# Layer 0 of a four-layer image kernel: two output blocks of a step joined, and the stage's last stores issued from three engines

## The chip, the cores and the metric

The kernel runs on one core of a Trainium2 chip, in one launch. The metric is the device time in microseconds. Several executions are timed and the median is given; one further execution is recorded by the hardware profiler.

## What is computed

The input is a batch of 4 images with 16 channels and 512 x 512 pixels. Four layers follow one another. The change is in layer 0, which is a window transformer block:

```python
x = x + depthwise3x3(x, pos_w) + pos_b
win = windows(affine(x), 8, 8)                 # 64 positions per window
q, k, v = split(win @ qkv_w.T + qkv_b)         # 2 heads of 8
out = softmax(q * 8**-0.5 @ k.T) @ v
x = x + (out @ proj_w.T + proj_b)              # back to image order
h1 = gelu(affine(x) @ fc1_w.T + fc1_b)         # 16 -> 64, exact gelu
x = x + (h1 @ fc2_w.T + fc2_b)                 # 64 -> 16
```

Layer 1 quantizes this x (for which it needs the largest absolute value), convolves it 3x3, normalizes it over the batch and clips it. Layer 2 is two 3x3 convolutions with a residual, layer 3 a 3x3 convolution with a two-layer pointwise network and a residual. Layers 1 to 3 are not touched.

## The kernel before

**Layer 0.** `window_attention` works in 64 steps (`STEPS`), numbered n. A step holds, for each of the 4 images (u) and each of 4 strips of rows (vv), eight 8x8 windows side by side: 512 positions. The 128 partitions are four quads of 32; a quad is a strip with two 16-channel halves. A pair of steps (2k, 2k+1) fills one tile `xo` of outputs, 128 columns wide, which is then stored to `x1` in DRAM, the input of layer 1.

All of PE, DVE, ACT and SP run in the order in which the program is written (a manual schedule); POOL is left to the framework. SP issues all DMAs of this stage: the input tiles (`load`), the turned keys (`turn_keys`, L318) and the stores (`_store_block`, L96). In a step the program goes through attention (`scores` L359, `attend` L378 and L383, `divide`, `values` L346), then `queries` of the next step, then `project` (L402, its sum on DVE at L407), and then the last part, which the change is in. There 52 places are filled in turn:

- every third place from the fifth on is a `hidden` (L416): four matmuls of 32x32 tiles for one image and strip, numbered q = 0 to 15 with u = q // 4, into bank 4 + q % 3, followed by the gelu on ACT (L421) into a tile `hid`;
- the other places are `depthwise` of step n + 2 (L295): four matmuls of 32x32 tiles for one tap of one image, into banks 0 to 3. The last two steps have none of it, as there is no step n + 2;
- `output` (L427): when the four hidden tiles of an image are there, four matmuls of 128x32 tiles with fc2 into bank 7, then an add of y on DVE into `xo` (L429) and, in odd steps, `store`: a maximum over xo on DVE (L438) and the store DMAs of that image.

`output` of image 0 stands behind hidden 5, that of image 1 behind hidden 9, that of image 2 behind the 52 places and after `position`, and that of image 3 in the next step, behind its first `scores`. `hid` has 8 buffers, used in turn. In the code:

```python
hids.append(hidden(y, q, n))
if q in (5, 9):
    output(y, xo, hids[q - 5 : q - 1], q // 4 - 1, n)
...
output(y, xo, hids[8:12], 2, n)
last = (y, xo, hids[12:], U - 1, n)
```

A PE instruction waits in order: if one waits for a semaphore, what is written behind it waits as well. In float32 each matmul shows as two records in the trace.

**The end of layer 0.** After step 63 the largest values are reduced on DVE and POOL (L523, L525), a bound is made of them, and every engine loads the resulting flag (L534) and branches: if the bound does not hold, a safer form of layer 0 (`attention_block`) would be run instead. With this input it is not. An odd step stores 16 DMAs for each image; in the last row of steps three of them are split in two, so step 63 has 19 for each image, 76 in all. Layer 1 begins with loads of `x1` (`_load_pairs`, L891), which need these stores.

Of the kernel before, what the change touches and what calls it, by code (L numbers as in the profile page):

```python
# [1 line left out]

# [9 lines left out]
F32 = mybir.dt.float32  # L12
BF16 = mybir.dt.bfloat16
AF = mybir.ActivationFunctionType
ALU = mybir.AluOpType
# [9 lines left out]
P = 128  # L25
# [6 lines left out]
WS = 8  # L32
# [51 lines left out]
        nc.sync.dma_start(part[:, at : at + m, :], src[:, a : a + m, :])  # L84


def _store_block(nc, x1, src, b, r0, cols):

    n = WS // 2
    s, m = divmod(r0 // 2, M)  # L90
    parts = [(1, m, s, 0, n), (0, m + 1, s, 0, n)]
    if m + n == M and s < S - 1:
        parts[1:] = [(0, m + 1, s, 0, n - 1), (0, 0, s + 1, n - 1, 1)]
    for r, mm, ss, at, k in parts:
        part = 32 * b + C * r
        nc.sync.dma_start(  # L96
            x1[mm : mm + k, part : part + C, ss, cols].rearrange("m c x -> c m x"),
            src.rearrange("c (m r) x -> c m r x", r=2)[:, at : at + k, 1 - r],
        )
# [53 lines left out]
def window_attention(ctx: ExitStack, tc, xw, x1, hots, m, v, peak):  # L153
# [14 lines left out]
    nc = tc.nc  # L168
    U = V = 4
    BW = 64  # L170
    NJ = BW // WS
    N = NJ * T
    XW = 2 * BW
    SR = H // 8
    NQ = W // XW
    STEPS = SR // WS * NQ * 2
# [7 lines left out]
    def bank(i):  # L184
        return pairs[i // 2][:, i % 2, :] if i < 4 else singles[i - 4]

    def quad(i):
        return slice(32 * i, 32 * i + 32)
# [82 lines left out]
    px = ctx.enter_context(tc.tile_pool(name="w0x", bufs=2))  # L271
# [12 lines left out]
    def by_window(ap):  # L284
        return ap.rearrange("p (j a x) -> p a j x", a=WS, x=WS)
# [29 lines left out]
    def turn_keys(y, vv):  # L315
        for u in range(U):
            for w in range(2):
                nc.sync.dma_start(  # L318
                    y2[32 * u + C * w : 32 * u + C * w + C, vv, :, w, :],
                    y[32 * vv + C * w : 32 * vv + C * w + C, u, :].rearrange(  # L320
                        "p (j t) -> p j t", t=T
                    ),
                )
# [17 lines left out]
    def values(k, n):  # L341

        vv, jl = k // 2, 4 * (k % 2)
        b = bank(4 + 2 * (k % 2))
        for jj in range(4):
            nc.tensor.transpose(  # L346
                b[:, P * jj : P * jj + P],
                y2[:, vv, jl + jj].rearrange("p w t -> p (w t)"), m("ident"),
            )
        t = px.tile([P, 4, P], F32, tag="yt", name=f"yt{n}_{k}", bufs=3)  # L350
        nc.vector.tensor_copy(t.rearrange("p j c -> p (j c)"), b)  # L351
        return t

    def scores(k, n):

        vv, jl = k // 2, 4 * (k % 2)
        for jj in range(4):
            for u in range(U):
                nc.tensor.matmul(  # L359
                    bank(u)[:, P * jj : P * jj + P],  # L360
                    y2[quad(u), vv, jl + jj].rearrange("p w t -> p (w t)"),
                    g[quad(u), vv, jl + jj].rearrange("p h t -> p (h t)"),
                    start=True, stop=True,
                )
        e = px.tile([P, U, 4, P], F32, tag="e", name=f"e{n}_{k}", bufs=3)
        for i in range(2):
            nc.scalar.activation(  # L367
                e[:, 2 * i : 2 * i + 2].rearrange("p u j t -> p u (j t)"),
                pairs[i], AF.Exp,
            )  # L370
        return e

    def attend(e, yt, k):

        b, d = bank(4 + 2 * (k % 2)), bank(5 + 2 * (k % 2))
        for jj in range(4):
            for u in range(U):
                nc.tensor.matmul(  # L378
                    b[quad(u), P * jj : P * jj + P], yt[:, jj, quad(u)], e[:, u, jj, :],
                    start=True, stop=True,  # L380
                )
        for u in range(U):
            nc.tensor.matmul(  # L383
                d[quad(u)], own, e[:, u].rearrange("p j t -> p (j t)"),
                start=True, stop=True,
            )

    def divide(k, n):
        vv, jl = k // 2, 4 * (k % 2)
        b, d = bank(4 + 2 * (k % 2)), bank(5 + 2 * (k % 2))  # L390
        r = px.tile([P, 512], F32, tag="r", name=f"r{n}_{k}")
        nc.scalar.activation(r, d, AF.Ln)
        nc.scalar.activation(r, r, AF.Exp, scale=-1.0)  # L393
        nc.vector.tensor_tensor(
            o[:, vv, jl : jl + 4].rearrange("p j h t -> p (j h t)"), b, r, ALU.mult
        )

    def project(y):
        for h in range(NH):
            for u in range(U):  # L400
                for vv in range(V):
                    nc.tensor.matmul(  # L402
                        bank(4 + u)[quad(vv)], wo[h][quad(u)], o[quad(u), vv, :, h, :],
                        start=h == 0, stop=h == 1,
                    )
        for u in range(U):
            nc.vector.scalar_tensor_tensor(  # L407
                y[:, u], bank(4 + u), pb, y[:, u], ALU.add, ALU.add
            )

    def hidden(y, q, n):

        u, vv = q // 4, 3 * q % 4
        b = bank(4 + q % 3)
        for k in range(4):
            nc.tensor.matmul(  # L416
                b[quad(k)], fc1[quad(vv), quad(k)], y[quad(vv), u, :],
                start=True, stop=True,
            )
        hd = px.tile([P, N], F32, tag="hid", name=f"hid{n}_{u}_{vv}", bufs=8)  # L420
        nc.scalar.activation(hd, b, AF.Gelu, bias=f1b)  # L421
        return vv, hd

    def output(y, xo, hids, u, n):
        b = bank(7)
        for vv, hd in hids:
            nc.tensor.matmul(b[quad(vv)], m("fc2"), hd, start=True, stop=True)  # L427
        at = BW * (n % 2)
        nc.vector.tensor_tensor(  # L429
            xo[:, u, :, at : at + BW].rearrange("p a (j x) -> p a j x", x=WS),  # L430
            by_window(b), by_window(y[:, u]), ALU.add,
        )
        if n % 2:
            store(xo, n // 2, u)

    def store(xo, k, u):
        i, cb = divmod(k, NQ)
        nc.vector.tensor_reduce(  # L438
            peak[:, U * k + u : U * k + u + 1], xo[:, u], AX.XY, ALU.max,
            apply_absolute_value=True,  # L440
        )
        for vv in range(V):
            for w in range(2):
                r = SR * (2 * vv + w) + WS * i
                _store_block(
                    nc, x1, xo[32 * vv + C * w : 32 * vv + C * w + C, u], u, r,
                    slice(XW * cb, XW * cb + XW),
                )

    ctx.enter_context(  # L450
# [16 lines left out]
    last, xo = None, None  # L467
    for n in range(STEPS + 1):
        if n < STEPS:
            nc.scalar.preload_act_table_set("natural_log_exp_and_others")  # L470
            yts = {0: values(0, n)}
            es = {0: scores(0, n)}
        if last:

            output(*last)
        if n == STEPS:
            break
        for k in range(1, 8):
            es[k] = scores(k, n)
            attend(es[k - 1], yts[k - 1], k - 1)  # L480
            yts[k] = values(k, n)
            divide(k - 1, n)
            if k == 3:
                nc.vector.tensor_reduce(
                    most[:, n : n + 1], ys[n], AX.XY, ALU.max, apply_absolute_value=True
                )
            if k % 2 and n + 1 < STEPS:
                turn_keys(ys[n + 1], k // 2)
        if n + 1 < STEPS:
            queries(ys[n + 1], 0)  # L490
        attend(es[7], yts[7], 7)
        divide(7, n)
        if n + 1 < STEPS:
            queries(ys[n + 1], 1)
        y = ys.pop(n)
        project(y)

        ahead = n + 2 < STEPS
        if ahead and n % 2 == 0 and n // 2 + 2 < STEPS // 2:
            xts[n // 2 + 2] = load(n // 2 + 2)  # L500
        if n % 2 == 0:
            xo = px.tile([P, U, WS, XW], F32, tag="xo", name=f"xo{n}", bufs=1)


        hids, taken = [], [0] * U
        for i in range(13 * 4):
            q, rest = divmod(i - 4, 3)
            if i >= 4 and rest == 0 and q < 16:
                hids.append(hidden(y, q, n))
                if q in (5, 9):  # L510
                    output(y, xo, hids[q - 5 : q - 1], q // 4 - 1, n)
            elif ahead:
                depthwise(n + 2, taken[i % 4], i % 4)
                taken[i % 4] += 1
        if ahead:
            ys[n + 2] = position(n + 2)
        output(y, xo, hids[8:12], 2, n)
        last = (y, xo, hids[12:], U - 1, n)

# [810 lines left out]
```

## Time and profile before

| | |
|---|---|
| median of 3 executions | 6609.31 us (6609.27 to 6616.03) |
| the profiled execution | 6619.37 us, span 6617.5 us |
| mean granted TensorE clock | 0.98 |
| PE busy | 6388.5 us (97%) |
| ACT busy | 4209.4 us (64%) |
| DVE busy | 3192.7 us (48%) |
| POOL busy | 5.9 us |
| DMA issues for stores to x1 (L96) | 2096 on SP, median 0.42 us each, 1.7 us to landing |
| matmuls of fc2 in layer 0 (L427) | 2048 records, median 617 ns |

Durations and places below come from the profiled execution, which took 10.1 us longer than the median of the three runs. "Busy" of PE is the time in which at least one matmul is in the array; many small tiles can be in it together, so a busy PE may still be partly idle. A line of the timeline gives the start, the length, the engine, the line of the program, the operation with its tiles, and how many instructions were merged; in square brackets stand the idle time ahead of it and what ended it. "Issue" there means that no semaphore of the trace explains the idle time.

### The profile page before, as it was taken

To read this page: it belongs to the slowest core of one execution; us is meant where nothing else is said; L and a number is where in the kernel's file an instruction comes from. 1 tells how busy PE (TensorE), PEld (TensorE's weight loads), DVE (VectorE), ACT (ScalarE), POOL (GpSimd) and SP (SyncE) were. 2 spreads that over 40 slices of the span, in tenths; PEclk is the share of its full clock that TensorE was granted. 3 is DMA by queue.
4 is the path that set the end of the run, shared out by engine and by line. 5 is a ranking of instruction groups with operands and counts; after the bars stand their busy time and mean duration, and the time that the engine had idled before them with its cause. 6 is when DMAs were issued, how large, how long until landed. Compare 5 with 4: busy or idle time off the path is not lost. (4 is left out here: it accounts for less than half of the span.)

```text
span 6617.5 us, 317160 instructions
## 1 busy us (share of the span) xinstructions
PE 6388.5 (97%) x146976; PEld 3295.4 (50%) x146976; DVE 3192.7 (48%) x4640; ACT 4209.4 (64%) x5738; POOL 5.9 (0%) x25
## 2 busy tenths in 40 slices
PE   8999999999999999999996689999999999999998
PEld 5555555555555555555553344444444444444443
DVE  3444444444444444444445944444444444444444
ACT  5777777777777777777774545554555555555553
POOL 0000000000000000000000000000000000000000
PEclk9999999999999999999997789999999999999999
DMA  3333232333333333333324722222222222222221
GB/s 81 65 67 76 57 75 59 73 60 72 60 72 60 72 61 70 62 70 62 70 44 165 275 85 79 79 79 76 76 78 78 78 78 75 75 79 79 79 63 47
DMA packets 544391, 515.30 MB, mean 78 GB/s; under 512 B 349008, under 2 KB 480208, under 8 KB 514384
## 3 DMA queue, kind: packets, MB, share of 16 engines
q1 hardware_dynamic: 542768, 494.52, 28.6%
q8 instruction: 1154, 18.91, 1.2%
q14 instruction: 181, 1.48, 0.1%
q10 hardware_dynamic: 288, 0.39, 0.0%
HBM read 225.87 MB, written 134.48 MB: 54 GB/s over the span
## 5 line engine op out<-in xcount | busy, mean ns | idle before, releaser
L1117 PE MATMUL tb<-y,mat 32*32 32x512 f32 x16384 | 1684.6, 597 | 14.0 <-ACT hid L1123 7.5
L1123 ACT ACTIVATE hid<-tb,vec 128x512 f32<-128x512 f32 x1280 | 877.0, 687 | 1231.0 <-PE tb L1117 1205.6
L1125 DVE TENSOR_SCALAR hid<-tb,vec 128x512 f32<-128x512 f32 x768 | 576.8, 751 | 1173.9 <-PE tb L1117 860.5
L367 ACT ACTIVATE e<-pair 128x1024 f32<-128x1024 f32 x1024 | 992.4, 1021 | 225.7 <-PE pair L359 225.0
L295 PE MATMUL pair<-x,taps 32*32 32x512 f32 x18432 | 968.1, 606 | 1.9 <-ACT y L306 1.3
L416 PE MATMUL bank<-y,fc_e 32*32 32x512 f32 x8192 | 878.4, 607 | 3.7 <-ACT hid L421 3.1
L421 ACT ACTIVATE hid<-bank,f1b 128x512 f32<-128x512 f32 x1024 | 679.3, 686 | 298.3 <-PE bank L416 284.6
L351 DVE COPY yt<-bank 128x512 f32<-128x512 f32 x512 | 353.7, 691 | 905.8 <-PE bank L346 905.5
L1117 PEld LDWEIGHTS tb<-y,mat 32*32 32x32 f32 x16384 | 500.3, 103 | 406.0 <-issue 242.8
L359 PE MATMUL pair<-g,y 32*128 32x128 f32 x16384 | 652.2, 285 | 39.7 <-ACT e L367 38.7
L908 PE MATMUL tb<-z,cw 32*32 32x512 f32 x12864 | 643.8, 603 | 4.0 <-ACT z L1054 3.4
L359 PEld LDWEIGHTS pair<-g,y 32*128 32x128 f32 x16384 | 541.4, 186 | 185.9 <-ACT e L367 108.8
L908 PE MATMUL tb<-x,cw 32*32 32x512 f32 x12480 | 632.0, 597 | 1.5 <-ACT z L1054 1.5
L908 PE MATMUL tb<-h,cw 32*32 32x512 f32 x12672 | 628.6, 601 | 1.8 <-ACT z L1054 1.5
L295 PEld LDWEIGHTS pair<-x,taps 32*32 32x32 f32 x18432 | 459.0, 103 | 288.8 <-issue 183.7
L908 PE MATMUL tb<-q,cq 32*32 32x512 bf16 x12672 | 446.5, 436 | 122.1 <-ACT q L987 97.9
L378 PE MATMUL bank<-e,yt 128*32 128x128 f32 x16384 | 555.3, 276 | 0.9 <-ACT r L393 0.9
L383 PE MATMUL bank<-e,hot 128*32 128x512 f32 x4096 | 534.4, 592 | 0.0
L1131 PE MATMUL tb<-hid,mat 128*32 128x512 f32 x4096 | 498.5, 605 | 0.9 <-DVE o L1137 0.9
L378 PEld LDWEIGHTS bank<-e,yt 128*32 128x32 f32 x16384 | 417.7, 109 | 108.1 <-DVE yt L351 52.8
L429 DVE TENSOR_TENSOR xo<-bank,y 128x512 f32<-128x512 f32 x256 | 177.1, 692 | 546.2 <-PE bank L427 544.4
L346 PEld LDWEIGHTS bank<-mat,y 128*128 128x128 f32 x2048 | 215.2, 141 | 430.2 <-issue 376.5
(150 smaller groups left out, 6608.8 us busy)
## 6 DMA issues: line engine op xcount, KB each, us to landing
tx<-x SPq DMA_DIRECT2D x128, 1024.0 KB, 5.2
x<-in_xw_dram SPq DMA_DIRECT2D x32, 2600.0 KB, 9.9
y<-y SPq DMA_DIRECT2D x2048, 32.0 KB, 2.2
xi<-x SPq DMA_DIRECT2D x1024, 64.0 KB, 2.8
out_dram<-o SPq DMA_DIRECT2D x64, 1024.0 KB, 4.1
x<-xo SPq DMA_DIRECT2D x2000, 32.0 KB, 1.7
tx<-x SPq DMA_DIRECT2D x4, 768.0 KB, 4.2
x<-xo SPq DMA_DIRECT2D x48, 24.0 KB, 1.6
```

The costliest lines, as they stand in the source:

```text
L295: nc.tensor.matmul(bank(u)[quad(vv)], taps[quad(u), tap, :], xts[n // 2][quad(u), vv, dy : dy + WS, at : at + BW], start=tap == 0, stop=ta ...
L359: nc.tensor.matmul(bank(u)[:, P * jj : P * jj + P], y2[quad(u), vv, jl + jj].rearrange("p w t -> p (w t)"), g[quad(u), vv, jl + jj].rearra ...
L367: nc.scalar.activation(e[:, 2 * i : 2 * i + 2].rearrange("p u j t -> p u (j t)"), pairs[i], AF.Exp,)
L378: nc.tensor.matmul(b[quad(u), P * jj : P * jj + P], yt[:, jj, quad(u)], e[:, u, jj, :], start=True, stop=True,)
L383: nc.tensor.matmul(d[quad(u)], own, e[:, u].rearrange("p j t -> p (j t)"), start=True, stop=True,)
L416: nc.tensor.matmul(b[quad(k)], fc1[quad(vv), quad(k)], y[quad(vv), u, :], start=True, stop=True,)
L421: nc.scalar.activation(hd, b, AF.Gelu, bias=f1b)
L908: nc.tensor.matmul(p[i][_quad(j)], weights[_quad(i), side, dx, :], src[side][_quad(i), j, dx : dx + W], start=side == 0 and dx == 0, stop= ...
L1117: nc.tensor.matmul(p[_quad(c)], w1[_quad(b), 1 - par, 32 * c : 32 * c + 32], inner(ys(mm + par))[_quad(b), s, :], start=True, stop=True,)
L1123: nc.scalar.activation(hd, p, AF.Relu, bias=v("l3_b1"))
L1125: nc.vector.tensor_scalar(hd, p, v("l3_b1"), 0.0, ALU.add, ALU.max)
L1131: nc.tensor.matmul(out_bank[_quad(b), :], w2[:, par], hd, start=par == 0, stop=par == 1)
```

## The change

`output` now takes two images at once where it is called within the 52 places: behind hidden 10, for image 1 (hidden 4 to 7) into bank 6 and then image 0 (hidden 0 to 3) into bank 7, eight matmuls in a row. The two adds, and in odd steps the two stores, follow in that order. The outputs of images 2 and 3 stay where they were. `hid` gets 12 buffers. The stores of the last pair of steps (k = 31, so those of step 63) take their issuing engine from a cycle of SP, ACT and POOL; all other stores stay on SP.

```diff
-def _store_block(nc, x1, src, b, r0, cols):
+def _store_block(nc, x1, src, b, r0, cols, queues=None):
...
-        nc.sync.dma_start(
+        (next(queues) if queues else nc.sync).dma_start(
...
-        hd = px.tile([P, N], F32, tag="hid", name=f"hid{n}_{u}_{vv}", bufs=8)
+        hd = px.tile([P, N], F32, tag="hid", name=f"hid{n}_{u}_{vv}", bufs=12)
...
-    def output(y, xo, hids, u, n):
-        b = bank(7)
-        for vv, hd in hids:
-            nc.tensor.matmul(b[quad(vv)], m("fc2"), hd, start=True, stop=True)
+    def output(y, xo, hids, us, banks, n):
+
+        for k, (vv, hd) in enumerate(hids):
+            nc.tensor.matmul(
+                bank(banks[k // 4])[quad(vv)], m("fc2"), hd, start=True, stop=True
+            )
         at = BW * (n % 2)
-        nc.vector.tensor_tensor(
-            xo[:, u, :, at : at + BW].rearrange("p a (j x) -> p a j x", x=WS),
-            by_window(b), by_window(y[:, u]), ALU.add,
-        )
-        if n % 2:
-            store(xo, n // 2, u)
+        for u, i in zip(us, banks):
+            nc.vector.tensor_tensor(
+                xo[:, u, :, at : at + BW].rearrange("p a (j x) -> p a j x", x=WS),
+                by_window(bank(i)), by_window(y[:, u]), ALU.add,
+            )
+            if n % 2:
+                store(xo, n // 2, u)
+
+
+    queues = itertools.cycle((nc.sync, nc.scalar, nc.gpsimd))
...
-                    slice(XW * cb, XW * cb + XW),
+                    slice(XW * cb, XW * cb + XW), queues if k == STEPS // 2 - 1 else None,
...
-                if q in (5, 9):
-                    output(y, xo, hids[q - 5 : q - 1], q // 4 - 1, n)
+                if q == 10:
+
+
+                    output(y, xo, hids[4:8] + hids[0:4], (1, 0), (4 + 8 % 3, 7), n)
...
-        output(y, xo, hids[8:12], 2, n)
-        last = (y, xo, hids[12:], U - 1, n)
+        output(y, xo, hids[8:12], (2,), (7,), n)
+        last = (y, xo, hids[12:], (3,), (7,), n)
```

In step 63 the 38 stores of images 1 and 0 go 13 to SP, 13 to ACT and 12 to POOL; those of image 2 go 6, 6 and 7, those of image 3 go 7, 6 and 6. In the order of ACT's program the first 13 stand between gelu 10 and gelu 11, the others behind gelu 15.

More of the change, by code (lines that the diff above doesn't have):

```diff
@@ L1 @@
+import itertools
 from contextlib import ExitStack
```

## The prediction

> **What bounds the kernel now.** I read the page's first part, then stages cut from the span, then the order of instructions around the edited lines. The page names TensorE:
>
> ```profile
> PE 6388.5 (97%) x146976; PEld 3295.4 (50%) x146976; DVE 3192.7 (48%) x4640; ACT 4209.4 (64%) x5738; POOL 5.9 (0%) x25
> ```
>
> Layer 0 runs to about 3560 us, in 64 steps of some 54 us. The page's chain of waits reaches back only into the convolution layers, so it says nothing on this stage. A table by stage does (us, then busy time of PE, PEld, DVE, ACT, POOL; clock; DMA share):
>
> ```profile
> 1000.00:2000.00 1000.00, 989.11 (x21908) 569.49 (x21904) 463.90 (x611) 775.97 (x1035) 0.00 (x0) 1.00 0.32 66
> ```
>
> PE is busy 989 of 1000 us at full clock. Matmul ends are modelled and overlap, so "busy" hides idle array; the starts tell more. The timeline of PE, then of its weight loads, then of DVE, around one step's output blocks:
>
> ```profile
> 1075.24 0.69 PE L416 MATMUL bank<-y,fc_e 32*32 32x512 f32 x4
> 1075.86 1.06 PE L427 MATMUL bank<-hid,mat 128*32 128x512 f32 x8
> 1076.85 0.66 PE L295 MATMUL pair<-x,taps 32*32 32x512 f32 x8
> ...
> 1080.25 1.07 PE L427 MATMUL bank<-hid,mat 128*32 128x512 f32 x8
> ...
> 1086.81 1.06 PE L427 MATMUL bank<-hid,mat 128*32 128x512 f32 x8
> ```
>
> ```profile
> 1074.78 0.23 PEld L416 LDWEIGHTS bank<-y,fc_e 32*32 32x32 f32 x8
> 1075.85 0.16 PEld L427 LDWEIGHTS bank<-hid,mat 128*32 128x32 f32 x8 [0.84 <-issue]
> 1076.85 0.15 PEld L295 LDWEIGHTS pair<-x,taps 32*32 32x32 f32 x12 [0.84 <-issue]
> ```
>
> ```profile
> 1077.01 0.69 DVE L429 TENSOR_TENSOR xo<-bank,y 128x512 f32<-128x512 f32 x1 [4.12 <-PE bank L427]
> ```
>
> Around each L427 block the weight loads stand still for 0.84 us, on both sides, with no semaphore named: the array empties before it goes from 32x32 tiles to 128x32 tiles, and again on the way back. From the block's start to the next small matmul is 0.99 us.
>
> The end of the layer has another bound, SP:
>
> ```profile
> 3516.80 38.39 SPq L96 DMA_DIRECT2D x<-xo  x76
> ...
> 3533.02 0.69 DVE L429 TENSOR_TENSOR xo<-bank,y 128x512 f32<-128x512 f32 x1 [0.88 <-PE bank L427]
> ...
> 3536.12 0.15 DVE L533 TENSOR_SCALAR flag<-bound 128x1 int32<-128x1 f32 x1
> ...
> 3559.76 37.05 SPq L891 DMA_DIRECT2D tx<-x  x13
> ```
>
> The last data are ready at 3533.7 and the flag at 3536.3, but SP issues its 76 stores until 3555.2 (one is 0.42 us, about 0.47 from one to the next, with a few long ones), and layer 1's first load comes 4.6 us after that.
>
> **What the Trainium skill says.** "TensorEngine Tiling (Array Packing)", Key Properties: changing the tiling mode, not merely the tile, drains TensorE. The trace agrees: 0.84 us without weight loads on each side. "DMA: Bandwidth & Descriptors", Issuing engines are not separate DMA queues: DMAs from scalar, sync and gpsimd share the same 16 engines, so several issuers save only the time to initiate. Issue is what binds here (DMA share 0.25 in 3536 to 3560). The same page, Anatomy of one DMA — SWDGE (gpsimd) path, gives about 2.0 us fixed for a GpSimd DMA, most of it the receipt, and its summary table about 1 us to the first byte; no DMA of this trace is issued from POOL, so none here shows it. For ACT the trace has a price: its two loads at the start took 0.40 and 0.45 us, while SP issued too.
>
> **The change, part by part.**
>
> *Blocks.* I call four matmuls of L295 or L416 on one row strip a slot; in two passes each it leaves 8 records. Between the first and second block lie 12 slots, 4.39 us; between second and third 20 slots, 6.56 us. Now the first block goes, 15 more slots run on behind the first 20, then comes one block of eight matmuls, then 17 slots. The fc2 work doesn't vanish: a block of 8 records takes 1.06 us against 0.62 for one, so a pass adds about 0.45, and the four moved matmuls lengthen the other block by two passes, 0.9 us. With p us per slot in an undisturbed run, the old stretch is 4.39 + 6.56 = 10.95 and the new one 15p + (4.39 + 5p) + 0.9: the saving is 5.66 - 20p. All hangs on p. The two distances above give (6.56 - 4.39)/8 = 0.271, saving 0.24. The run ahead of the first block, from hidden 2 (1072.57) to hidden 5 (1074.79), gives 2.22/9 = 0.247, saving 0.72. The depthwise prelude at full clock (28.3 to 34.6, 214 records less about 19 in flight at an edge) gives 6.3/195 x 8 = 0.258, saving 0.50. I take the last. The first 62 steps have depthwise work: **31 us** (15 to 45). Drains alone would suggest much more; most of a block's 4.39 us is work that stays.
>
> *Gelu and banks.* Hidden 6 to 10 come without a break, one in 3 x 0.258 = 0.77 us; an L421 gelu is 0.69, so ACT keeps up. hid gets 12 buffers: hidden 0 to 10 fit. The block's first half writes bank 6, which gelu 8 must have left; its hidden is two hiddens ahead, as gelu 7 was for the old second block. Hidden 11 wants bank 6 again, after DVE's add. Before, the add started 1.15 us after its block and took 0.69: free at +1.84. Hidden 11 comes at 0.99 + 0.9 for the block, plus 0.05 for two slots: +1.94. Cover 0.1 us; I take no wait, at worst 0.1 x 62 = 6 us. If it waits, everything behind it on PE waits. The first add (u = 0) moves behind add u = 1 and its reduction, and the 32 stores of both images go to SP together in odd steps, 15 us of a queue that is next wanted for keys in the following step: nothing. xo is first written later than before, so its old stores are no later cover than they were.
>
> *Step 62* has no depthwise work; there a break holds the gelus up by 3.0 us (3514.87 to 3517.91 in its twin, step 63). One break less, a longer other: **1.5 us** (0 to 3).
>
> *Stores of step 63.* SP gets 26, ACT 25, POOL 25. Worked from the old step 63: gelus come three in 2.74 us, so gelu 10 ends near 3519.7, the block starts near 3519.2, add u = 1 ends near 3521.9 (1.94 + 0.69 after), add u = 0 near 3523.9. ACT then issues 13 stores ahead of gelu 11: 13 x 0.47 to 3528.0. Gelus 11 to 15 end at 3531.3, add u = 2 at 3533.2, add u = 3 at 3536.0, 2.3 us later than now. SP then has 7 stores left, to 3539.3, not the end any more. POOL is: its 25 stores start at 3521.9 and stand ahead of the reduction (L525) that makes the flag. At 1.0 us each, my estimate from the skill's page, they end at 3546.9; the flag takes 1.1 (3535.18 to 3536.27 before), layer 1 another 4.6: 3552.6 against 3559.76, **7 us** saved. At SP's 0.47, 15 us; at 2.0, 18 us lost; even at about 1.3.
>
> **Sum:** 31 + 1.5 + 7 = 39.5. The profiled execution took 6619.4 (span 6617.5), so 6579.9 of it; it stood 10.1 above the median of 6609.3, so about **6570**.
>
> **Rivals.**
> 1. *Work, not drains:* p stays at 0.271, 62 x 0.24 = 15; with 1.5 and 7: 6586. For: it is the pace next to the blocks. Against: the prelude.
> 2. *The wide gain:* p of 0.247 and a POOL as quick as SP: 45 + 3 + 15: 6546.
> 3. *POOL gates:* 2 us a store; 31 + 1.5 - 18: 6595. For: its queue alone holds the flag. Against: the skill's page puts most of the 2 us after issue.
> 4. *Slower:* the add u = 1 is let go only when the whole block is done. It then starts 0.9 later, hidden 11 comes at +2.79 against 1.94, and PE, in order, loses up to 0.85 in each of 62 steps: 53 - 31 - 8.5 = 13 us slower, 6623. It decides from a wait of 0.64 a step (39.5/62). Against: the two halves are waited for apart in the compiled order.
> 5. The output blocks do move in the compiled order, so a change without effect is only the rivals cancelling.
>
> **How the numbers follow.** Forecast 0.42, rival 1 0.20, rival 2 0.15, rival 3 0.13, rival 4 0.07, cancelling 0.03. A measurement can tell about 0.2%, 13 us, so faster means below 6596. Forecast, 1 and 2 lie there, and half of 3: 0.84. Same: half of 3 and the cancelling, 0.09. Slower 0.07. The range runs from just beyond rival 2 to past rival 3: 6543 to 6601.
>
> **What would show it.** Three L427 blocks a step instead of four, one with 16 records; the distance from its start to the third block near 4.39 + 5 x 0.258 + 0.9 = 6.6 us; the step 0.5 us shorter; no wait of L416 on DVE's xo. At the end, POOL's stores spaced near 1 us and layer 1's load about 16.6 us after the last add (now 26.1). If the step is not shorter, p is wrong or bank 6 is late; if the gap at the end is longer than now, it is POOL.

## The result and the profile after

The changed kernel takes 6591.28 us (median of 9 runs, 6583.26 to 6596.14). The kernel before, run beside it, takes 6616.37 us (6609.27 to 6620.79). The ratio is 0.9962 with a 95% interval of 0.9952 to 0.9972: 25 us less. The profiled execution took 6596.14 us (span 6594.3), against 6619.37 (6617.5) before.

TensorE is still what the page names:

```profile
PE 6374.4 (97%) x146976; PEld 3369.2 (51%) x146976; DVE 3195.1 (48%) x4640; ACT 4221.1 (64%) x5738; POOL 18.9 (0%) x50
```

The timeline of PE around the output blocks of one step (start, length, engine, line, operation, count). L428 is the old L427, L417 the old L416, L296 the old L295:

```profile
1074.59 1.92 PE L428 MATMUL bank<-hid,mat 128*32 128x512 f32 x16
...
1081.53 1.06 PE L428 MATMUL bank<-hid,mat 128*32 128x512 f32 x8
...
1084.26 1.07 PE L428 MATMUL bank<-hid,mat 128*32 128x512 f32 x8
```

Three blocks instead of four, the first of 16 records. Its start lies 6.94 us ahead of the next block's. The weight loads of the same place, and the adds on DVE:

```profile
1074.59 0.16 PEld L428 LDWEIGHTS bank<-hid,mat 128*32 128x32 f32 x8 [0.84 <-ACT hid L422]
...
1076.45 0.18 PEld L296 LDWEIGHTS pair<-x,taps 32*32 32x32 f32 x16 [0.84 <-issue]
```

```profile
1075.78 1.49 DVE L433 TENSOR_TENSOR xo<-bank,y 128x512 f32<-128x512 f32 x2 [7.95 <-ACT hid L422]
```

The pause of 0.84 us on each side of a block is as long as before; there is one pair of them less. (The profile books the first one here to the last gelu that the block needs; it is exactly as long as those for which it names no semaphore.) The first add starts 1.19 us after the block, as soon as its half of the block allows, and nothing in the step waits for it.

The end of layer 0, all engines, with what an engine waited for in square brackets:

```profile
3497.95 21.21 SPq L97 DMA_DIRECT2D x<-xo  x26
3497.96 7.36 ACTq L97 DMA_DIRECT2D x<-xo  x13
...
3498.23 6.30 POOL L97 DMA_DIRECT2D x<-xo  x12 [3476.70 <-DVE xo L433]
...
3505.37 1.84 ACT L422 ACTIVATE hid<-bank,f1b 128x512 f32<-128x512 f32 x3 [9.37 <-DMA x<-xo]
3506.11 2.51 PE L417 MATMUL bank<-y,fc_e 32*32 32x512 f32 x16 [5.94 <-ACT hid L422]
...
3513.37 0.69 DVE L433 TENSOR_TENSOR xo<-bank,y 128x512 f32<-128x512 f32 x1 [0.88 <-PE bank L428]
...
3518.19 0.31 POOL L534 PARTITION_ALL_REDUCE ytop<-top  x1
3518.53 0.27 DVE L539 TENSOR_SCALAR bound<-bound,ytop,sized 128x1 f32<-128x1 f32 x1 [3.02 <-POOL ytop L534]
...
3519.09 0.15 DVE L542 TENSOR_SCALAR flag<-bound 128x1 int32<-128x1 f32 x1
```

Three things are to be seen. Twelve stores on POOL take 6.30 us, 0.52 each, about SP's pace. ACT issues its 13 first stores ahead of gelu 11, so the gelus stand still for 9.37 us and PE for 5.94. And the last add ends at 3514.07, the flag at 3519.24, and layer 1's first load starts at 3525.10: 11.0 us after the last add, where it was 26.1.

In stages, by the two traces:

| | before | after | difference |
|---|---|---|---|
| one step (mean of 61) | 54.19 | 53.79 | -0.40 |
| end of the last add | 3533.71 | 3514.07 | -19.6 |
| layer 1's first load | 3559.76 | 3525.10 | -34.7 |
| from there to the end (layers 1 to 3) | 3057.7 | 3069.2 | +11.5 |

In this pair of traces layer 0 gains 34.7 us, near the forecast of 39.5. But layers 1 to 3, which the change doesn't touch, take 11.5 us longer. Where that comes from was the question for the experiments.

### The profile page after: what moved, and what is told of

It reads as the page before. It is cut to its first block, busy times and chain, and to the rows that moved or that the text cites. A ratio compares the mean times of both kernels' runs of the same rounds, so it can differ in the third digit from the quotient of the medians.

```text
span 6594.3 us, 316838 instructions
## 1 busy us (share of the span) xinstructions
PE 6374.4 (97%) x146976; PEld 3369.2 (51%) x146976; DVE 3195.1 (48%) x4640; ACT 4221.1 (64%) x5738; POOL 18.9 (0%) x50
## 5 line engine op out<-in xcount | busy, mean ns | idle before, releaser
L1126 PE MATMUL tb<-y,mat 32*32 32x512 f32 x16384 | 1696.1, 597 | 10.7 <-ACT hid L1132 7.7
L296 PE MATMUL pair<-x,taps 32*32 32x512 f32 x18432 | 963.6, 605 | 2.9 <-ACT y L307 1.3
L417 PE MATMUL bank<-y,fc_e 32*32 32x512 f32 x8192 | 840.5, 607 | 7.3 <-ACT hid L422 6.7
L1126 PEld LDWEIGHTS tb<-y,mat 32*32 32x32 f32 x16384 | 503.5, 103 | 393.6 <-issue 229.3
L360 PE MATMUL pair<-g,y 32*128 32x128 f32 x16384 | 636.9, 284 | 39.5 <-ACT e L368 38.7
L296 PEld LDWEIGHTS pair<-x,taps 32*32 32x32 f32 x18432 | 526.0, 103 | 226.5 <-issue 102.4
L360 PEld LDWEIGHTS pair<-g,y 32*128 32x128 f32 x16384 | 526.6, 186 | 185.3 <-ACT e L368 108.8
```

Source lines behind the costliest of these rows:

```text
L296: nc.tensor.matmul(bank(u)[quad(vv)], taps[quad(u), tap, :], xts[n // 2][quad(u), vv, dy : dy + WS, at : at + BW], start=tap == 0, stop=ta ...
L360: nc.tensor.matmul(bank(u)[:, P * jj : P * jj + P], y2[quad(u), vv, jl + jj].rearrange("p w t -> p (w t)"), g[quad(u), vv, jl + jj].rearra ...
L417: nc.tensor.matmul(b[quad(k)], fc1[quad(vv), quad(k)], y[quad(vv), u, :], start=True, stop=True,)
L1126: nc.tensor.matmul(p[_quad(c)], w1[_quad(b), 1 - par, 32 * c : 32 * c + 32], inner(ys(mm + par))[_quad(b), s, :], start=True, stop=True,)
```

## The experiments

**Each part alone, and both kernels again.** The joined block with all stores on SP:

```diff
-                    slice(XW * cb, XW * cb + XW), queues if k == STEPS // 2 - 1 else None,
+                    slice(XW * cb, XW * cb + XW), None,
```

> The joined block alone; all stores stay on SP. The trace of the changed kernel has a step 0.45 us shorter than before (54.11 to 53.66 us) and layers 1 to 3 11.5 us longer (3069.2 instead of 3057.7 us from the first tx load to the end). If the blocks are worth what the steps show: layer 0 shorter by about 62 x 0.45 = 28 us, the gap from the last add to layer 1's first load as before (26 us) or a little longer. Theory A, the lengthening of layers 1 to 3 comes with the stores on ACT and POOL: they take 3058 us here, in all about 28 us less than before. Theory B, it comes with the new order of blocks: 3069 us, in all about 17 us less. Theory C, it varies from execution to execution: either, and the median some 22 us less. The rival that joining saves nothing: no change of the steps.

The stores on three engines with the old blocks (`hid` with 8 buffers, no joined output):

```diff
-                if q == 10:
-                    output(y, xo, hids[4:8] + hids[0:4], (1, 0), (4 + 8 % 3, 7), n)
+                if q in (5, 9):
+                    output(y, xo, hids[q - 5 : q - 1], (q // 4 - 1,), (7,), n)
```

> The stores of step 63 on three engines alone; output blocks and hid buffers as before. Steps of 54.1 us. The gap from the last add to layer 1's first load was 26.05 us before and 11.04 us in the changed kernel; ACT's stores delay gelus by some 5 us in step 63. So layer 0 ends about 8 to 11 us earlier. Theory A: layers 1 to 3 take 3069 us, in all no gain or up to 3 us lost. Theory B: 3058 us, in all 8 to 11 us less. Theory C: either, median about 4 us less.

The two kernels once more, for the spread of the stages on this chip:

> The kernel before once more, for a second profile. Theories A and B: layers 1 to 3 take 3058 us again, within 1 us. Theory C: they may take up to 3069 us.

> The changed kernel once more, for a second profile. Theories A and B: layers 1 to 3 take 3069 us again, within 1 us. Theory C: they may take down to 3058 us. Layer 0 to the first tx load: 3525 us.

| | time, us | ratio to before | layers 1 to 3 |
|---|---|---|---|
| joined block alone | 6592.68 (6590.66 to 6595.83) | 0.9963 [0.9950, 0.9977] | 3051.2 |
| stores alone | 6617.67 (6609.23 to 6631.06) | 1.0002 [0.9994, 1.0010] | 3068.1 |
| before, once | 6609.51 | | 3054.6 |
| changed, once | 6594.15 | | 3069.3 |

So the joined block alone gains as much as the whole change, 24.5 us of medians. The stores alone bring nothing, although layer 1's first load follows the last add by 11.0 us there too. Layers 1 to 3 take 3051 to 3058 us with the stores on SP and 3068 to 3069 with the stores on three engines.

Two readings go with this table. The stages of a single trace are good to some 5 us: in the second pair of profiles layer 1's first load comes 30.1 us earlier (3523.09 against 3553.14), not 34.7, and layers 1 to 3 take 14.7 us longer, not 11.5. And with all stores on SP the joined block makes the end of layer 0 longer, by its one trace. Counted from the first copy of `yt` in step 63 (L351 before, number 504 counting from 0; "copy 504" below), layer 1's first load comes after 92.1 us with the joined block alone, after 88.0 and 85.0 in the two profiles of before, and after 77.0 and 77.2 in those of the changed kernel.

**What lengthens layers 1 to 3.** Setting the two traces side by side, DVE instruction by instruction, most of the difference comes in jumps of some 0.8 us, fifteen of them (12.2 us together), one every 168.5 us. At these places PE's weight loads pause without a semaphore in both kernels. The first line is of before, the next two of after:

```profile
4118.80 0.13 PEld L1117 LDWEIGHTS tb<-y,mat 32*32 32x32 f32 x5 [1.13 <-issue]
```

```profile
4085.16 0.10 PEld L917 LDWEIGHTS tb<-z,cw 32*32 32x32 f32 x1 [1.23 <-issue]
4085.16 0.12 PEld L1126 LDWEIGHTS tb<-y,mat 32*32 32x32 f32 x3
```

The pause is nearly as long in both. But in the kernel before it falls ahead of a whole group of four L1117 matmuls, one for each strip; in the changed one it falls elsewhere, and of the matmuls of L1126 three start and the fourth comes late. The matmuls of PE behind the pause, before and then after:

```profile
4118.81 0.63 PE L1117 MATMUL tb<-y,mat 32*32 32x512 f32 x4 [0.23 <-issue]
```

```profile
4085.16 0.61 PE L917 MATMUL tb<-z,cw 32*32 32x512 f32 x1 [0.32 <-issue]
4085.16 0.62 PE L1126 MATMUL tb<-y,mat 32*32 32x512 f32 x3
...
4086.04 0.58 PE L1126 MATMUL tb<-y,mat 32*32 32x512 f32 x1
```

In the compiled programs PE's executed instructions are the same in number. But the branch to `attention_block`, which is not entered, has 32646 instructions for PE instead of 32642: with POOL's stores in the program, PE waits for four more semaphores there. All of PE's code for layers 1 to 3 behind it moves by four. (The branch grows by four for the other engines as well.) The theory "place of the code" says that this alone costs the 11 us; the rival "queues" says that stores on POOL or ACT leave something behind. The first kernel for it is the kernel before with one matmul more in the branch that is not entered. It moves PE's code alone. In float32 that is also four instructions, as the trace shows two weight loads and two matmuls for each:

```diff
         nc.tensor.matmul(pk, wk, chunk(xw, k), start=True, stop=True)
+        for _ in range(1 if (i, k) == (0, 0) else 0):
+            nc.tensor.matmul(pk, wk, chunk(xw, k), start=True, stop=True)
```

> The kernel before with one more matmul in the attention branch, which this input never enters: nothing that is executed differs from the kernel before. In the program it moves all of TensorE's code for layers 1 to 3 by four instructions, as much as the changed kernel's branch grew (four waits more, for the POOL stores in it). Theory 'place of the code': layers 1 to 3 (first load of layer 1 to the end) take 3069 us as in the changed kernel, not 3055, and the kernel is 11 to 16 us slower than before, near 6630. Rival 'queues' (stores on the ACT and POOL queues leave something behind that slows layers 1 to 3): no difference from before, 6616 and 3055.

The changed kernel with 15 such matmuls in another function of the same branch, so that together with the four waits 64 instructions are added (4 + 15 x 4); it is called the padded kernel below:

```diff
     def project(xw, o, n, k):
...
+        for _ in range(15 if n == f"{NB-1}_{NC-1}" else 0):
+            nc.tensor.matmul(pp, wp[:, 0], o[:, :, 0, :], start=True, stop=True)
```

> The changed kernel with 15 repeated matmuls in the branch that is not entered, 64 instructions of TensorE's with the four waits, so that the code of layers 1 to 3 lies as in the kernel before, but for 64 instructions; nothing that is executed differs from the changed kernel. 'Place of the code', with a pattern that repeats every 64 instructions: layers 1 to 3 back at 3051 to 3058 us, near 6581 in all. 'Queues': 3069 and 6594 as before.

The changed kernel with stores on two engines, whose branch has its old size of 32642:

```diff
-    queues = itertools.cycle((nc.sync, nc.scalar, nc.gpsimd))
+    queues = itertools.cycle((nc.sync, nc.scalar))
```

> The changed kernel with the stores of step 63 on SP and ACT alone. Without POOL stores the branch has its old size and the code its old place. 'Place of the code': layers 1 to 3 at 3051 to 3058 us; ACT holds 19 stores ahead of gelu 11 instead of 13, about 10 us, so layer 1's first load comes at 3527 to 3531, and the kernel takes 6580 to 6590. 'Queues' (a second hardware queue is enough): 3069, near 6598.

And the changed kernel with 7 matmuls more at the place of the first diff. They bring one wait more, so that the code moves by 4 + 7 x 4 + 1 = 33:

> The changed kernel with 7 repeated matmuls in the branch that is not entered: the code of layers 1 to 3 lies 33 instructions behind that of the kernel before (mod 64), a third place. 'Place of the code': layers 1 to 3 take another time than 3069, somewhere in 3045 to 3075, with TensorE's unexplained stalls at other instructions. 'Queues': 3069.

| | code moved by | layers 1 to 3 | time, us | ratio to before |
|---|---|---|---|---|
| before, one matmul more | 4 | 3066.7 | 6631.19 (6618.38 to 6635.24) | 1.0016 [1.0008, 1.0025] |
| changed, 15 more | 64 | 3054.3 | 6580.81 (6576.38 to 6585.46) | 0.9948 [0.9934, 0.9961] |
| changed, SP and ACT | 0 | 3050.4 | 6582.34 (6575.68 to 6588.47) | 0.9948 [0.9935, 0.9962] |
| changed, 7 more | 33 | 3051.8 | 6575.91 (one run) | |

One matmul that is never executed makes the kernel before slower by 0.16%, with all its stores on SP. Moving the code by 64 takes the changed kernel from 0.9962 to 0.9948 of before; the intervals of these two still touch, so the stage shows it better than the total. "Queues" falls: POOL's stores are all there in the padded kernel.

The totals of layers 1 to 3 mix in something else. Their first 470 to 477 us and their last 127 to 134 us vary from trace to trace, for the same kernel too (474.1 and 470.4 for the first part in the two profiles of before). Between them, from PE's weight load 60,000 to its load 2,000 (counted back from the end of the program), all traces of this document fall into three groups:

| code moved by | kernels | this stretch, us |
|---|---|---|
| 4 | changed (both profiles), stores alone, before with one matmul more | 2465.4 to 2466.4 |
| 0 or 64 | before (both profiles), joined block alone, SP and ACT, padded, and the three kernels further below | 2453.3 to 2454.6 |
| 33 | changed, 7 more | 2447.9 |

The pause moves as the code does. Counted back in the same way, the first one after 4080 us stands ahead of load 58,008 in the kernels whose code lies at its old place, and ahead of load 58,010 in those moved by four, so two loads and their two matmuls earlier. In those moved by 64 it stands ahead of load 57,016, which is 58,008 - 8 x 128 + 32: earlier by 32 loads and their matmuls, but for a whole number of 128 loads. So its places lie on one fixed grid of 128 loads with their matmuls, 256 instructions, over which the code slides. In the kernel moved by 33 no pause longer than 0.85 us is left in this part; why is not shown.

The trace of the kernel before with one matmul more shows the pause in the changed kernel's form:

```profile
4121.60 0.10 PEld L910 LDWEIGHTS tb<-z,cw 32*32 32x32 f32 x1 [1.11 <-issue]
4121.61 0.11 PEld L1119 LDWEIGHTS tb<-y,mat 32*32 32x32 f32 x3
```

The groups of weight loads from 4080 to 6400 us carry the same sign. These are the rows of `tb<-z,cw` of before, of after and of before with one matmul more (busy and mean, then idle time ahead and what ended it); the changed kernel with 15 more has 187.9 idle, 100.2 of it "issue", as before:

```profile
L908 PEld LDWEIGHTS tb<-z,cw 32*32 32x32 f32 x10560 | 221.7, 103 | 188.0 <-issue 100.0 <-DVE x L1084 61.0
```

```profile
L917 PEld LDWEIGHTS tb<-z,cw 32*32 32x32 f32 x10598 | 225.0, 103 | 205.4 <-issue 113.7 <-DVE x L1093 61.0
```

```profile
L910 PEld LDWEIGHTS tb<-z,cw 32*32 32x32 f32 x10583 | 225.1, 103 | 204.5 <-issue 112.3 <-DVE x L1086 61.0
```

These rows don't show the loss itself: the pause is booked to the load that ends it, and the row of `tb<-y,mat` falls from 330.4 us of idle time before to 316.7 after. They show which load that is, the same one in the changed kernel and in the kernel before with its code moved by four.

That PE pauses there to fetch instructions is argued and not shown. For it: a stretch of 168.5 us holds 3968 weight loads and as many matmuls, 7936 instructions, which are 31 blocks of 256; and the page lists transfers of the kind "instruction" of 16 KB each:

```profile
q8 instruction: 1154, 18.91, 1.2%
```

The Trainium skill, "Runtime: NRT & Kernel Launch", Instruction fetch mechanics, has the instruction memory refilled in 16 KiB blocks of 256 instructions, and calls the cost of crossing a boundary mostly hidden. The block size fits this trace, and so does the number of transfers: by the page's figure, PE's 146976 weight loads and as many matmuls would fill 1148 blocks, an estimate. If the pause is such a crossing, its cost is not hidden here: which instruction the boundary falls on decides about 12 us of the 2454.

**What holds up step 63.** In the padded changed kernel, images 1 and 0 are stored by SP and POOL only, image 2 by ACT, image 3 by SP and POOL:

```diff
-    queues = itertools.cycle((nc.sync, nc.scalar, nc.gpsimd))
+    pair = itertools.cycle((nc.sync, nc.gpsimd))
+    one = itertools.repeat(nc.scalar)
+    queues = (pair, pair, one, pair)
```

> The changed kernel with the padded branch (code of layers 1 to 3 where it lay before) and another division of step 63's stores: images 1 and 0 on SP and POOL alone, image 2 on ACT, image 3 on SP and POOL. If ACT's 13 stores ahead of gelu 11 are what holds up step 63, gelu 11 follows gelu 10 by under 2 us instead of 10, the last add comes 6 to 8 us earlier, SP and POOL carry 19 stores each from the joined block on (19 x 0.51 = 9.7 us) and then 9 or 10 of image 3's (5 us), and layer 1's first load comes 2 to 5 us earlier: about 6577. If gelu 11 waited for something else, no change from the padded kernel: 6581.

It takes 6578.52 us (6575.27 to 6587.18; 0.9944 [0.9931, 0.9958]), which the runs can't tell from the padded kernel. In the trace, gelu 11 and the stores:

```profile
3498.82 18.85 SPq L97 DMA_DIRECT2D x<-xo  x29
...
3499.10 14.43 POOL L97 DMA_DIRECT2D x<-xo  x28 [3478.05 <-DVE xo L433]
...
3501.08 3.19 ACT L422 ACTIVATE hid<-bank,f1b 128x512 f32<-128x512 f32 x5 [4.22 <-PE bank L417]
```

ACT's stores are gone from ahead of gelu 11, which now follows gelu 10 by 4.9 us instead of 10.0. The expected 2 us is missed since gelu 11 then waits for PE, where the joined block (3.64 us here) stands ahead of its hidden layer. From copy 504 the last add ends after 59.6 us instead of 65.1, but layer 1's first load comes after 75.7 instead of 76.3. SP, with 29 stores until 3517.67, has become the last to issue, so ending ACT's hold-up wins almost nothing.

**A second joined block.** Does the gain of the change repeat? Images 2 and 3 in one block at the start of the next step, in the padded changed kernel:

```diff
-        output(y, xo, hids[8:12], (2,), (7,), n)
-        last = (y, xo, hids[12:], (3,), (7,), n)
+        last = (y, xo, hids[8:], (2, 3), (6, 7), n)
```

> The padded changed kernel with images 2 and 3 also in one block, on banks 6 and 7, at the start of the next step. It takes away a block between the hidden layer (32x32 tiles) and the values (128x128), where one change of tile remains: so one drain of about 0.52 us goes each step, 63 x 0.52 = 33 us, if a drain costs PE its gap wherever it stands. The joined block of the change gained 0.45 us a step for a pair of drains, by which ratio 15 us. So 6545 to 6566. Rival: PE waits in the block for gelu 15 or the scores for the adds, and the gain is eaten: 6575 or more. The tail of step 63 gets 2 to 3 us longer, since image 2's stores start later.

It takes 6583.89 us (6582.57 to 6586.89; 0.9953 [0.9939, 0.9967]): nothing gained. The step is 53.78 us, and 53.77 in the padded kernel. The rival holds, though its cause is ACT. PE at the start of a step:

```profile
3390.86 0.66 PE L347 MATMUL bank<-mat,y 128*128 128x128 f32 x4 [0.16 <-ACT hid L422]
3391.49 0.49 PE L360 MATMUL pair<-g,y 32*128 32x128 f32 x4
3392.27 1.16 PE L360 MATMUL pair<-g,y 32*128 32x128 f32 x28 [0.28 <-ACT y L307]
3393.36 1.92 PE L428 MATMUL bank<-hid,mat 128*32 128x512 f32 x16
```

The values wait for the last gelu, which reads bank 4, and the scores for `position` on ACT (L307). On ACT three gelus, L307, a table load and the first exponential follow one another without a gap; from the first of these gelus to the exponential it is 4.66 us in the padded kernel (3387.19 to 3391.85) and 4.67 in this one (3388.86 to 3393.53). At this place ACT sets the pace, and the block that was taken away there had cost nothing.

**Both together.** The second joined block, and images 1 and 0 stored by SP and POOL, 2 and 3 by all three:

> Images 2 and 3 in one block as in the second kernel, and the stores of step 63 for images 1 and 0 on SP and POOL, for 2 and 3 on all three engines. If both effects stand by themselves, 3 to 6 us below the second kernel.

It takes 6579.82 us (6577.33 to 6582.92; 0.9945 [0.9931, 0.9958]), 4.1 below the second joined block alone, as expected, though the two intervals overlap. In the trace layer 1's first load comes 73.3 us after copy 504, against 76.3 in the padded kernel: the shortest end of layer 0, without a measurable gain over that kernel. In the traces of this kernel and of the first of the three, layers 1 to 3 take 3060.7 us, 6.4 more than in the padded one; by the stretches above, all of it lies in their first and last parts, which vary.

The padded kernel, the one with SP and ACT, and the first and last of these three all lie at 0.9944 to 0.9948 of before and aren't told apart. The plainest of them is the changed one with POOL taken out of the cycle. It is clear of the kernel before, and below the changed kernel in the median, though these two intervals touch (0.9935 to 0.9962 and 0.9952 to 0.9972).

## Why the prediction was right, and where not

The forecast was 6570 us, with 6543 to 6601; the result is 6591, faster, as the forecast said. Its sum of 39.5 us stands against 25 of medians (23 by the two traces), and rivals 1 and 3, with 6586 and 6595, lie nearer to the result than the forecast does. Point by point:

1. **Blocks, 31 us: right in kind, 24 in size.** Copy 504 comes at 3448.12 instead of 3471.81, 23.7 us earlier; a step is 0.40 us shorter in the mean and 0.46 by the medians of the distances between its blocks, against 0.50. But the size is in part luck. The 15 slots that now run undisturbed take 3.80 us more in the long stretch (43.99 against 40.19): p is 0.253, against 0.258 forecast. From the joined block to the third it is 6.93 us, not the 6.58 worked out. The block itself takes what was worked out, 1.85 us until the next small matmul against 0.99 + 0.9. The 17 slots behind it take 5.08 us, about 0.35 more than was put down for them; why is not shown. These two give 10.95 - 3.80 - 6.93 = 0.22 a step, 14 us in 62 steps. That is what rival 1 said, though its reason fell: the slots that run on undisturbed do go faster than 0.271. Another 0.24 a step was not in the sum at all: from the third block to the fourth it is 2.73 us instead of 2.97. There, in the step shown, the scores of before stretch to 1.50 us while ACT works on L306; after, ACT is done with the last gelu earlier and the scores take 1.21. Before, on ACT and on PE, and then after:

```profile
1087.42 1.26 ACT L306 ACTIVATE y<-pair,vec 128x512 f32<-128x512 f32 x2
```

```profile
1088.39 1.50 PE L359 MATMUL pair<-g,y 32*128 32x128 f32 x32
```

```profile
1081.65 1.47 ACT L307 ACTIVATE y<-pair,vec 128x512 f32<-128x512 f32 x2
...
1083.11 1.21 PE L360 MATMUL pair<-g,y 32*128 32x128 f32 x32
```

*Step 62*, put at 1.5 us saved, shows no saving: 54.89 us against 54.30, and 50.17 in the second profile of before.

2. **No wait on bank 6: right.** In the 62 steps with depthwise work the weight loads of L417 wait for DVE's add a single time, for 0.26 us. With it rival 4, the slower side, falls. The first add starts with the block still running, as the rival's counter-argument had it.

3. **Stores, 7 us: right in sign, 11 at layer 1's first load, and mis-sized in POOL's price.** Two terms made it: a last add 2.3 us later, and a gap behind it of 16.6 us. Counted from copy 504, the last add ends 4.1 us later (65.95 against 61.90), so ACT's hold-up was foreseen but undersized; this figure is loose, since the second profile of before has 55.1 us there, and by it the gain at layer 1's first load is 7.8 us, not 11. The gap is 11.0, as POOL was put at 1.0 us a store, from the Trainium skill ("DMA: Bandwidth & Descriptors", Anatomy of one DMA — SWDGE (gpsimd) path, and its table Specifications), and its stores took 0.51 to 0.53. That page's time runs to the first byte; the trace shows POOL free for its next store sooner. So POOL does not gate alone. Its reduction (L534, for which DVE waits 3.02 us) starts when its last store is issued, at 3518.16, and the flag is there at 3519.24, while SP issues its last store until 3519.17: the two end together. Layer 1's first load comes 5.9 us later, where the forecast took 4.6 from before; the kernels with POOL's stores have 5.5 to 7.0 us there and those without 4.3 to 4.9, and the cause of that is not shown. Rival 3's 2 us a store falls, so its 6595 lies near the result by chance. Rival 2 had POOL as quick as SP, rightly, but its total of 6546 needed every term at its widest.

4. **What failed is a term that was missing: layers 1 to 3.** The sum took for granted that what is not touched keeps its time. It lost 11.5 us there, all that the stores had won, since the POOL stores lengthened a branch that is never entered by four instructions. No rival had it either. With the code moved by 64 instead of 4, the changed kernel takes 6581, 11 us from the forecast. So the forecast was right on the direction and on the range, but its sum was neither complete nor right term by term.

## What to carry to other kernels

A pause of PE's at a change of tile is worth removing only where PE sets the pace: in this kernel the same joining brought 0.4 us a step amid PE's own work and nothing at the step's border, where ACT's chain ends last. Before a time is credited to an edit, compare the stages that it doesn't touch; if they jump by a fixed amount at regular distances, look at what the edit did to the place of the code. Stores that an engine issues stand in its program order: give them to an engine with nothing behind them.

## What the runs showed of the hardware

The place of PE's code is worth 11 to 13 us in a stretch of 2454: moved by four instructions, the middle of layers 1 to 3 took 2465.4 to 2466.4 us, moved by 0 and 64 it took 2453.3 to 2454.6, and moved by 33 it took 2447.9 in the one trace there is. A store issued by POOL takes 0.51 to 0.53 us of its queue, hardly more than the 0.47 of SP alone. While SP, ACT and POOL issue together, SP's stores lie 0.56 us apart and ACT's 0.58 in the changed kernel.
